# Clearing the value blocks in DRAM ahead of the key load of batch 1 instead of inside the loop: a graph-attention kernel on one Trainium2 core

## The chip, the core and the metric

The kernel runs on one core of one Trainium2 chip. The metric is the device time in microseconds (us) of one execution, as the median of three runs. Beside the runs there is one profiled execution, from which all rows and durations come. In its rows PE is TensorE (PEld its weight loads), DVE is VectorE, ACT is ScalarE, POOL is GpSimd and SP is SyncE, which here only issues DMAs.

## The reference

Sixteen batches (B = 16) of N = 512 nodes with F = 512 features go through a graph attention in two directions (`adj` as it is and transposed), with H = 16 heads of 32 features. Only the first 20 nodes (`NONGT`) serve as keys and values. All is float32.

```python
q_exp = where(row_zero, 0, q)                       # row_zero: x.sum(-1) == 0
self_feat = concat([x, q_exp]) @ W_self.T + b_self
out = self_feat
for d in range(2):
    A = adj (d == 0) or its transpose, [:, :, :20, :]       # 11 labels
    cond, vb = A.sum(-1), A @ w_bias + b_bias
    kv = self_feat[:, :20]
    aff = (self_feat @ Wq.T + bq) . (kv @ Wk.T + bk) / sqrt(32)   # per head
    w = softmax(where(cond > 0, aff, -9e15) + vb)
    out = out + (w @ kv) @ Wout[head].T + bout
return x + relu(out)
```

## The kernel before

**Set-up.** The first 92 us load all weights and compute, for all 16 batches at once, what hangs only on the 320 key nodes: `keys` (L551) makes from keys and query weights one matrix per batch, 512 x 640 (16 heads x 40 columns: 20 nodes in 2 directions), and writes it to DRAM: `g1_d` for batch 1 (L585), `g_d` for batches 2 to 15 (L586); that of batch 0 stays in SBUF (`g0`). `values` (L525) makes the values times the output weights and writes them to `vw_d`.

**Value blocks.** The attention weights of a node tile are turned with 32x32 transposes, so a head's 40 columns do not lie on the borders of the blocks of 32. `bd_d` in DRAM holds, for each batch, the values laid out to fit: 32 rows, 4 heads of a group, 2 blocks each, 128 numbers. The rows that hold no value of the head must be zero. `clear_blocks` (L121) writes those zeros for all batches, in six DMAs (L129) of 128 to 384 pieces of 512 bytes, 768 KB in all. `blocks` (L134) copies the values from `vw_d` into the other rows, in twelve DMAs (L145) of the same pieces. The two write different rows. `load_values` (L113) reads the blocks of one batch into SBUF in four DMAs (L117).

**The loop.** It runs over the batches b, and in each over four tiles of 128 nodes, nt = 0 to 3. All engines follow the order in which the program was written (`manual_schedule`); nothing is sorted by a planner. For a tile:

- PE: `self_feat` (L189) parts of this batch or the next, 16 matmuls each, into a bank of the pool `ps_acc`, which has four banks; then `scores` (L254), 32 matmuls with the keys of the batch (`load_keys`, L111); in nt = 2 of every batch b > 0 also `attend` (L321) for batch b - 1, 128 small matmuls with `vd`, which need all four banks of `ps_acc`.
- DVE: `self_copy` (L202) empties a `self_feat` bank into SBUF, `weigh` (L265, L267, L269) adds masks and subtracts the maximum, `normal` (L301, L302) sums, `turn` (L310) transposes. For the masks, `mask_count` (L216, L217) counts labels and `mask_add` (L223, L225) adds the bias.
- ACT: exponentials (L274), `mask_mul` (L210) turns the integer masks into floats, copies (L230).
- POOL: multiplies masks by the label weights (L211), adds masks and key bias (`full_add`, L239), scales the exponentials (L303).

The masks of a batch come in two halves, `adj(b,0)` and `adj(b,1)` (L96); the bias of keys is `cq(b)` (L103, two DMAs). In b = 1 the first work on `adj(1,1)` is in nt = 0.

**The DMA queue of SP.** Nearly all transfers are issued by SP, in program order. Around the change the order is: the last writes of `g1_d` and `g_d`; then, at the head of the loop, the keys of batch 1; in b = 0, nt = 1 `adj(1,0)`, `cq(1)`, the six clears, the twelve blocks; in nt = 2 the values of batch 0, `x(2)` (L88), `adj(1,1)`, two halves of `xn(2)` (L92), then `adj(2,0)` and `cq(2)`. The lines of the program:

```python
if nt == 1:
    if b + 1 < B:
        load_adj(b + 1, 0)
        load_cq(b + 1)
    if b == 0:
        clear_blocks(zero)
        blocks()
if nt == 2:
    load_values(b)
```

Each DMA signals its end on one of eight semaphores, taken in turn.

Of the kernel before, what the change touches and what calls it, by code (L numbers as in the profile page):

```python
# [18 lines left out]
def gat_kernel(  # L19
# [53 lines left out]
    zero = const.tile([32, P], F32, name="zero")  # L73
# [20 lines left out]
    def load_adj(b, h):  # L94
        t = adjs[b, h] = load.tile([P, 2, S * L], I32, tag="adj", name=f"adj{b}_{h}", bufs=3)
        nc.sync.dma_start(  # L96
            t, adj[b, h * 2 * P : (h + 1) * 2 * P].rearrange("(t p) d m l -> p t (d m l)", p=P)
        )

    def load_cq(b):  # L100
        cqs[b] = load.tile([P, H // 2, S], F32, tag="cq", name=f"cq{b}")
        for a in range(2):
            nc.sync.dma_start(  # L103
                cqs[b][bass.ts(a, R)].rearrange("p h m -> p (h m)"),
                cq_d[b : b + 1, bass.ts(a, H // 2)].rearrange("b h d m -> b (h d m)").partition_broadcast(R),
            )

    def load_keys(b):
        gs[b] = gp.tile([P, C, W], F32, tag="g", name=f"g{b}")
        src = g1_d if b == 1 else g_d[:, :, b - 2]  # L110
        nc.sync.dma_start(gs[b].rearrange("p c (a w) -> p (c a) w", a=C), src.rearrange("x p w -> p x w"))  # L111
# [9 lines left out]
    def clear_blocks(zero):  # L121

        for e in range(HL):
            for i in range(2):
                j = (e * S) // 32 + i
                lo, hi = max(e * S, 32 * j) - 32 * j, min(e * S + S, 32 * j + 32) - 32 * j
                for a, z in ((0, lo), (hi, 32)):
                    if a < z:
                        nc.sync.dma_start(  # L129
                            bb[:, a:z, e, i].rearrange("b r w -> r b w"),  # L130
                            zero[: z - a].unsqueeze(1).to_broadcast([z - a, B, P]),
                        )

    def blocks():  # L134

        vv = vw_d.rearrange("d (b m) (e w) -> d b m e w", m=NG, e=HL)
        for e in range(HL):
            for i in range(2):
                j = (e * S) // 32 + i
                for d in range(2):  # L140
                    lo = max(e * S + d * NG, 32 * j)
                    hi = min(e * S + (d + 1) * NG, 32 * j + 32)
                    if lo < hi:
                        m, r = lo - e * S - d * NG, lo - 32 * j
                        nc.sync.dma_start(bb[:, r : r + hi - lo, e, i], vv[d, :, m : m + hi - lo, e])  # L145
# [506 lines left out]

    gs[0] = g0
    with tc.manual_schedule():
        load_keys(1)

        def side(t, lo, hi, q):
# [16 lines left out]
        for b in range(B):  # L674
# [13 lines left out]
            for nt in range(NT):  # L688
                store()
                if nt == 1:  # L690
                    if b + 1 < B:
                        load_adj(b + 1, 0)
                        load_cq(b + 1)
                    if b == 0:
                        clear_blocks(zero)
                        blocks()
                if nt == 2:
                    load_values(b)
# [182 lines left out]
```

## Time and profile before

| | |
|---|---|
| runs | 630.17, 630.88, 630.75 us: median 630.75 |
| profiled execution | 630.1 us, its span (first to last instruction) 627.1 us |
| granted TensorE clock | 1.00 |
| PE busy | 619.6 us (99%) |
| DVE busy | 506.2 us (81%) |
| POOL busy | 342.1 us (55%) |
| ACT busy | 217.9 us (35%) |
| chain that ended last | PE 97%, DMA 1% |
| SP's DMA queue | 128.61 MB, 61.8% of what 16 DMA engines can do in the span |

A row of the timeline has the start and the duration in us (of all instructions that it merges), engine, line, operation, output<-inputs, shapes, the number of instructions, and in brackets the idle time of the engine before it with what ended it. SP's rows are the time that it takes to issue a DMA; the transfer goes on behind it, and the time from issue to landing is given apart.

### The profile page before, as it was taken

To read this page: it belongs to the slowest core of one execution; us is meant where nothing else is said; L and a number is where in the kernel's file an instruction comes from. 1 tells how busy PE (TensorE), PEld (TensorE's weight loads), DVE (VectorE), ACT (ScalarE), POOL (GpSimd) and SP (SyncE) were. 2 spreads that over 40 slices of the span, in tenths; PEclk is the share of its full clock that TensorE was granted. 3 is DMA by queue.
4 is the path that set the end of the run, shared out by engine and by line. 5 is a ranking of instruction groups with operands and counts; after the bars stand their busy time and mean duration, and the time that the engine had idled before them with its cause. 6 is when DMAs were issued, how large, how long until landed. Compare 5 with 4: busy or idle time off the path is not lost.

```text
span 627.1 us, 16412 instructions
## 1 busy us (share of the span) xinstructions
PE 619.6 (99%) x6830; PEld 380.3 (61%) x6830; DVE 506.2 (81%) x809; ACT 217.9 (35%) x480; POOL 342.1 (55%) x268
## 2 busy tenths in 40 slices
PE   8999999999999999999999999999999999999997
PEld 6654558866565656565565656565656565655654
DVE  1377657789888888888888979798888888888896
ACT  1445422133242424241524334332424242415341
POOL 2406332537556474738292847465564747382974
PEclk9999999999999999999999999999999999999999
DMA  8999998629284655738391919393757657492513
GB/s 303 399 393 320 360 389 247 219 76 304 102 251 154 188 219 120 286 97 310 56 350 33 334 45 290 112 289 116 232 174 186 220 135 271 87 320 49 184 36 135
DMA packets 88976, 131.53 MB, mean 210 GB/s; under 512 B 8808, under 2 KB 59016, under 8 KB 86856
## 3 DMA queue, kind: packets, MB, share of 16 engines
q1 hardware_dynamic: 87656, 128.61, 61.8%
q0 software_dynamic: 672, 1.36, 0.9%
q8 instruction: 53, 0.87, 0.6%
q10 hardware_dynamic: 576, 0.53, 0.3%
q14 instruction: 19, 0.16, 0.1%
HBM read 90.89 MB, written 39.92 MB: 209 GB/s over the span
## 4 chain that ended last, share of the span: by engine, by line
PE 97%; DMA 1%; issue 0%; SPq 0%; DVE 0%; ACT 0%; DVEq 0%
PE ps_s L254 44%; PE ps_sf L189 34%; PE ps_o L321 7%; PE ps_v L533 3%; PE ps_k L480 3%; DMA ws_q<-in_wsT 1%; PE ps_kv L431 1%; PE ps_o L667 1%; PE ps_nz L172 0%; PE ps_c L511 0%; PE ps_g(0, 3, 0, 0, 2)0_367 L560 0%; PE ps_q L441 0%; PE ps_g(1, 3, 1, 0, 2)0_530 L560 0%; PE ps_g(1, 1, 0, 1, 2)0_436 L560 0%; PE ps_g(3, 3, 0, 0, 2)0_799 L560 0%
## 5 line engine op out<-in xcount | busy, mean ns | idle before, releaser
L254 PE MATMUL ps_s<-g,sf 128*64 128x320 f32 x2048 | 287.5, 433 | 0.5 <-ACT st L575 0.5
L254 PEld LDWEIGHTS ps_s<-g,sf 128*64 128x64 f32 x2048 | 152.0, 137 | 119.9 <-issue 6.6
L189 PE MATMUL ps_sf<-x,ws_v 128*64 128x256 f32 (+1 forms) x2048 | 222.1, 371 | 0.0
L189 PEld LDWEIGHTS ps_sf<-x,ws_v 128*64 128x64 f32 x2048 | 151.5, 137 | 67.5 <-issue 2.6
L303 POOL TENSOR_TENSOR s<-s,sm 128x640 f32<-128x640 f32 x63 | 80.1, 1272 | 138.4 <-DVE sm L302 138.4
L274 ACT ACTIVATE s<-s 128x640 f32<-128x640 f32 x63 | 46.5, 738 | 214.4 <-DVE s L269 214.4
L239 POOL TENSOR_TENSOR full<-cq,both 128x640 f32<-128x640 f32 x64 | 99.0, 1547 | 25.2 <-ACT both L230 23.5
L211 POOL TENSOR_TENSOR prod<-prod,wb_sb 128x880 f32<-128x880 f32 x32 | 61.3, 1916 | 55.2 <-ACT prod L210 55.2
L265 DVE TENSOR_TENSOR ps_s<-ps_s,full 128x640 f32<-128x640 f32 x63 | 52.3, 830 | 38.6 <-PE ps_s L254 37.1
L343 POOL TENSOR_TENSOR o<-o,x 128x512 f32<-128x512 f32 x60 | 75.6, 1279 | 1.1 <-ACT o L340 1.1
L230 ACT COPY both<-add 64x80 f32<-64x80 f32 x128 | 32.8, 256 | 77.4 <-DVE add L225 76.3
L340 ACT ACTIVATE o<-o,bo 128x512 f32<-128x512 f32 x60 | 40.0, 714 | 44.3 <-DVE o L334 44.3
L301 DVE TENSOR_REDUCE sm<-s 128x32 f32<-128x640 f32 x63 | 51.6, 819 | 4.5 <-ACT s L274 0.9
L267 DVE TENSOR_REDUCE mx<-ps_s 128x32 f32<-128x640 f32 x63 | 52.0, 825 | 2.2
L269 DVE TENSOR_TENSOR s<-ps_s,mx 128x640 f32<-128x640 f32 x63 | 51.9, 824 | 2.2
L202 DVE SCALAR_TENSOR_TENSOR sf<-nz,qw,ps_sf 128x236 f32<-128x236 f32 (+1 forms) x128 | 52.6, 459 | 1.1 <-PE ps_sf L189 1.0
L310 DVE STREAM_TRANSPOSE wt<-s 128x640 f32<-128x640 f32 x63 | 52.6, 834 | 0.2 <-POOL s L303 0.2
L321 PE MATMUL ps_o<-wt,vd 32*32 32x256 f32 (+2 forms) x2176 | 45.8, 372 | 1.1 <-issue 1.1
L321 PEld LDWEIGHTS ps_o<-wt,vd 32*32 32x32 f32 x2176 | 30.2, 103 | 16.9 <-issue 8.5
L334 DVE TENSOR_TENSOR o<-ps_o,sf 128x512 f32<-128x512 f32 x60 | 36.3, 668 | 0.0
L152 ACT ACTIVATE xn<-xn 128x512 f32<-128x512 f32 x56 | 34.3, 613 | 0.0
L216 DVE TENSOR_REDUCE cond<-adj 128x80 f32<-128x880 int32 x32 | 33.2, 1037 | 1.2 <-DMA adj<-in_adj 1.2
(213 smaller groups left out, 423.1 us busy)
## 6 DMA issues: line engine op xcount, KB each, us to landing
g<-g_d SPq DMA_DIRECT2D x15, 1280.0 KB, 9.1
g_d<-st SPq DMA_DIRECT2D x16, 1120.0 KB, 6.4
x<-in_xT SPq DMA_DIRECT2D x16, 1024.0 KB, 11.0
out_T<-o SPq DMA_DIRECT2D x60, 256.0 KB, 4.3
xn<-in_xn SPq DMA_DIRECT2D x28, 512.0 KB, 8.5
adj<-in_adj SPq DMA_DIRECT2D x32, 440.0 KB, 7.2
vd<-bd_d SPq DMA_DIRECT2D x64, 128.0 KB, 4.0
nz<-nz_d SPq DMA_DIRECT2D x14, 256.0 KB, 4.9
```

The source lines that it names most:

```text
L189: nc.tensor.matmul(held[0][bass.ts(a, R), i * N // 2 : i * N // 2 + hi - lo], ws_v[:, k, bass.ds((2 * f + i) * P + a * R, R)], xs[b][:, k, ...
L202: nc.vector.scalar_tensor_tensor(sfs[b][:, 2 * f + i, lo:hi], nzs[b][:, lo:hi], qw[:, 2 * f + i, b : b + 1], ps[:, i * N // 2 : i * N // 2 ...
L211: nc.gpsimd.tensor_mul(p, p, wb_sb.unsqueeze(1).to_broadcast([P, 2 * S, L]))
L239: nc.gpsimd.tensor_add(f, cqs[b].unsqueeze(1).to_broadcast(shape), adds[b, nt // 2][:, nt % 2].unsqueeze(2).to_broadcast(shape),)
L254: nc.tensor.matmul(bank[bass.ts(a, R), : W // 2], sfs[b][:, k, bass.ds(nt * P + g * R, R)], keys[:, k, a], start=start and k == 0, stop=(k ...
L265: nc.vector.tensor_add(pw, pw, fulls.pop((b, nt)).rearrange("p g h m -> p g (h m)"))
L267: nc.vector.tensor_reduce(mx, p4, AX.X, ALU.max)
L269: nc.vector.tensor_sub(s, p4, mx.unsqueeze(3).to_broadcast(full))
L303: nc.gpsimd.tensor_mul(s, s, sm.unsqueeze(3).to_broadcast(full))
L310: nc.vector.transpose(wts[b][:, nt], s.rearrange("p a h m -> p (a h m)"))
L321: nc.tensor.matmul(banks[q][bass.ts(e, DH)].rearrange("p (t n) -> p t n", n=32), vds[b][r, e, i, q // 2 * 2 + n], wt[r, :, bass.ts(j, 32)] ...
L343: nc.gpsimd.tensor_add(o[:, c], o[:, c], xs[b][:, c])
```

## The change

`clear_blocks(zero)` is called at the head of the loop's section, before the keys of batch 1 are loaded, and no longer in b = 0, nt = 1. `blocks()` stays where it is. The six clears are the same; on SP they now stand ahead of the keys of batch 1, `adj(1,0)` and the two DMAs of `cq(1)`.

```diff
     gs[0] = g0
     with tc.manual_schedule():
+        clear_blocks(zero)
         load_keys(1)
 
         def side(t, lo, hi, q):
...
                         load_adj(b + 1, 0)
                         load_cq(b + 1)
                     if b == 0:
-                        clear_blocks(zero)
                         blocks()
                 if nt == 2:
                     load_values(b)
```

## The prediction

> **What bounds the kernel now.** First the page:
>
> ```profile
> span 627.1 us, 16412 instructions
> PE 619.6 (99%) x6830; PEld 380.3 (61%) x6830; DVE 506.2 (81%) x809; ACT 217.9 (35%) x480; POOL 342.1 (55%) x268
> ```
>
> TensorE (PE) is busy for 619.6 of 627.1 us at a granted clock of 1.00, and the chain that ended last is 97% PE. A moved DMA can therefore change the time only where PE itself stands still. From the point of the edit (92 us) on, PE's rows show one such place inside the loop, and one only (the other, 0.48 us, is in the tail): the first `attend`, of batch 0, in b = 1, nt = 2. Below it stands the same step one batch later (start us, duration us, group, idle before):
>
> ```profile
> 134.44 0.63 PE L321 MATMUL ps_o<-wt,vd 32*32 32x256 f32 x6
> 135.66 2.70 PE L321 MATMUL ps_o<-wt,vd 32*32 32x256 f32 x122 [0.58 <-issue]
> ...
> 168.94 2.75 PE L321 MATMUL ps_o<-wt,vd 32*32 32x256 f32 x128
> ```
>
> From the first `attend` matmul to the scores after it (138.28) batch 0 takes 3.84 us; one batch later it is 168.94 to 171.62, 2.68 us. The stall costs **1.16 us**. The fourth accumulator bank is what is missing: PE's sequencer waits 3.33 us in one place of L321, up to 135.60, when VectorE (DVE) has emptied that bank with the last L202. So DVE's rows come next:
>
> ```profile
> 123.37 0.35 DVE L302 RECIPROCAL sm<-sm 128x32 f32<-128x32 f32 x1
> 124.97 1.07 DVE L216 TENSOR_REDUCE cond<-adj 128x80 f32<-128x880 int32 x1 [1.25 <-DMA adj<-in_adj]
> 126.08 1.93 DVE L217 TENSOR_SCALAR cond<-cond 128x80 f32<-128x80 f32 x1
> 127.93 0.86 DVE L202 SCALAR_TENSOR_TENSOR sf<-nz,qw,ps_sf 128x256 f32<-128x256 f32 x2
> 128.71 0.82 DVE L265 TENSOR_TENSOR ps_s<-ps_s,full 128x640 f32<-128x640 f32 x1
> ...
> 134.69 0.86 DVE L202 SCALAR_TENSOR_TENSOR sf<-nz,qw,ps_sf 128x256 f32<-128x256 f32 x2
> ```
>
> From 124.97 to 135.55 DVE has no idle time. It entered this stretch late, because L216 waited 1.25 us for the masks `adj(1,1)`. And L217 took 1.93 us where the other batches show 0.51: it ended just after GpSimd's (POOL's) L211 (126.03 to 127.95), which it met only because it was late. Last the SP queue, which issues those masks:
>
> ```profile
> 92.03 0.32 SPq L586 DMA_DIRECT2D g_d<-st  x1
> 94.48 0.37 SPq L111 DMA_DIRECT2D g<-g_d  x1
> 94.91 2.27 SPq L96 DMA_DIRECT2D adj<-in_adj  x1
> 97.22 1.18 SPq L103 DMA_DIRECT2D cq<-cq_d  x2
> 98.44 6.12 SPq L129 DMA_DIRECT2D bd_d<-zero  x6
> 104.67 8.87 SPq L145 DMA_DIRECT2D bd_d<-vw_d  x12
> 116.60 1.72 SPq L117 DMA_DIRECT2D vd<-bd_d  x4
> 118.36 0.43 SPq L88 DMA_DIRECT2D x<-in_xT  x1
> 118.84 0.50 SPq L96 DMA_DIRECT2D adj<-in_adj  x1
> ```
>
> SP goes through this without a pause but two: 92.35 to 94.48, where the key load L111 waits for the last write of `g1_d`, and 113.54 to 116.60, where L117 waits for the blocks. The last row is `adj(1,1)`: issued at 118.84, landed 6.1 us later, at 124.95.
>
> **The change, part by part.** No instruction is added or removed; six DMAs (`clear_blocks`, L129) pass three loads (keys of batch 1, `adj(1,0)`, `cq(1)`: four DMAs) on SP. From the first block (L145) on the order of all queues is as before.
>
> *Clears earlier.* They need only `zero`, set at 0.7 us. They start at 92.40, in the 2.1 us in which SP waited. The program also makes each SP DMA wait for the landing of the one eight places before it; for the sixth clear that is a `g_d` write landed at 94.12, for the others it has landed by 91.5. Their SP time lies between 6 x 0.31 = 1.9 us (the shortest of the six) and the 6.12 us of before: they end between about 94.4 and 98.5.
>
> *Keys, `adj(1,0)`, `cq(1)` later.* Counted on SP, the keys are issued at 98.5 at the latest instead of 94.48: 4.0 us later. Counted on the DMA engines, which are full at that time (share 1.04 in 96 to 100, 320 GB/s), the 768 KB (786 kB) of clears go ahead: at 257 GB/s (the window 102 to 103, in which they ran before) 3.1 us, at 320 GB/s 2.5 us. I take 3.2 us, bounds 2.5 and 4.0. The keys landed before `cq(1)`, which landed at 103.3 at the latest; shifted, they come by 107, and PE first reads them at 122.21: 15 us of cover, cost nothing. `cq(1)` is read at 117.41 by POOL: nothing. `adj(1,0)`, in by 103.3 before, comes at 106.5 (105.8 to 107.3). ScalarE reads it at 107.34, DVE at 108.59; a delay there would first use up DVE's idle time of 1.48 us at 117.62. Cost nothing.
>
> [...]
>
> *Blocks earlier, with new neighbours.* Through the same rule of eight, block 5 now waits for the keys and block 6 for `adj(1,0)`, where both waited for older transfers. So SP, free for the blocks at about 101 to 102, does the first four and stops at block 5 and 6: block 6 starts with the landing of `adj(1,0)`, at 106.5. Before, the trace has it at 109.05. The blocks 6 to 12 follow at 0.60 to 0.64 us each as before, so that everything behind is **2.5 us earlier** (1.8 to 3.2): values L117, `x(2)`, and `adj(1,1)`, which lands at 122.4 (121.7 to 123.2).
>
> *What that is worth.* L216 needs its masks when the reciprocal of 123.37 is through, at 123.64. With 122.4 the 1.25 us of idle time are gone. L217 then starts at 124.7 and waits for POOL's L303 alone (to 125.14), as in later batches, not for L211; it ends at 125.2, and L202 at 126.0. L265 no longer waits for DVE but for PE's scores, which end at 126.75: it starts at 126.85 in place of 128.71, 1.86 us earlier. The rest of the stretch keeps its length (128.71 to 135.55, 6.84 us) and ends at 133.7, ahead of PE's need at 134.44. If L217 met L211 all the same (125.14 to 127.06 then), L265 would start at 127.8, 0.9 us earlier, and 0.25 us of the stall would stay. I take the first, since four later batches that I looked at have L217 at 0.51.
>
> So the stall of 1.16 us goes, and no more can be had: PE is then without a pause up to the tail. Behind it PE's chain moves as a whole, since from b = 2 on no `attend` has such a pause. SP itself next waits at 122.6 to 140.3 for the row flags of DVE, so the 2.5 us of SP end there.
>
> **Sum.** Profiled execution of before: 630.1 us, span 627.1. Minus 1.16: span 625.9, execution 628.9. The median of the three runs, 630.75, lies 0.65 above the profiled execution: 630.75 - 1.16 = **629.6 us**.
>
> **Rivals.**
>
> *A: nothing is gained.* If `adj(1,0)` lands at 109.05, block 6 and all behind stand where they stood, and the time is 630.75. Against it: that takes 5.7 us of delay, where SP's own count gives at most 4.0. For it: the four DMA issues behind the clears may be held up as L96 was (2.27 us) by 1536 packets more in the queue, and the blocks may be slower than 0.6 us while the keys still run.
>
> *B: slower, through block 6.* The mechanism is the new wait of block 6 for `adj(1,0)`: from a landing at 109.05 on, each us of delay is a us for `adj(1,1)`, for L216 and for the bank that PE waits for. It happens if the clears get through the queue at less than 786 kB / 5.7 us = 137 GB/s. In 104 to 108, when half of them ran before, the core's DMA engines moved 114 GB/s: 6.9 us, landing at 110.2, the stall 1.2 us longer, 631.9 us. At the slowest us (104 to 105, 72 GB/s) 10.9 us, landing at 114.2, 5.2 us longer, 635.9 us. Against it: in those windows the DMA share was 0.52 and 0.36, the queue waited for SP, while at 92 it is full and SP is ahead of it.
>
> That the change does not do what it says is no case: the order of SP is fixed by hand.
>
> **Numbers.** A measurement of this kernel can tell about 0.2% from no change, 1.26 us. The gain of 1.16 us stands 0.1 us short of that line, and the three runs of before spread over 0.71 us, so the main case falls on both sides almost evenly. Main case 0.75: 0.36 faster, 0.39 same. A 0.12: 0.11 same, 0.01 slower. B 0.10: 0.09 slower, 0.01 same. Left over 0.03: 0.01 faster, 0.02 slower. That makes faster 0.37, same 0.51, slower 0.12. The range starts at the main case less 0.6 for the spread, 629.0, takes in the gain of 0.9 and rival A with half the spread, 631.1, and leaves B out.
>
> **What would show it.** In the profile after: L129 from 92.4, L111 between 95 and 98.5; L145 from about 101, with a pause before its fifth or sixth DMA; L117 at about 114 in place of 116.60; no "DMA adj" in front of the L216 that follows, L217 there at 0.5 us; the first L321 in one piece of 2.7 us; a span near 625.9. Wrong it is if L117 is not at least 1.3 us earlier, if L217 still takes 1.9 us, or if PE waits at L321 though DVE is early.

## The result: 0.3% slower

The changed kernel takes 632.44 us, the kernel before 630.31 us (medians of 21 executions each). The ratio is **1.0032**, with a 95% interval of 1.0021 to 1.0043: 1.3 to 2.7 us lost, where 1.16 us of gain was forecast. The profiled execution took 632.8 us:

```profile
span 630.2 us, 16411 instructions
PE 620.2 (98%) x6830; PEld 380.8 (60%) x6830; DVE 507.8 (81%) x809; ACT 218.5 (35%) x480; POOL 342.4 (54%) x268
```

PE's busy time has grown by 0.6 us only; the span by 3.1. The rows of PE at the first `attend` show nearly all of it (start, duration, group, idle before):

```profile
134.70 0.63 PE L321 MATMUL ps_o<-wt,vd 32*32 32x256 f32 x6
137.45 4.03 PE L321 MATMUL ps_o<-wt,vd 32*32 32x256 f32 x122 [2.13 <-issue]
```

The stall has not gone but grown, from 0.58 to 2.13 us of idle time. And the 122 matmuls behind it take 4.03 us in place of 2.70. The table by stage tells why (us, then busy time and instructions of PE, PEld, DVE, ACT and POOL, then the granted clock of PE, the DMA share and GB/s):

```profile
136.00:138.00 2.00, 0.55 (x32) 0.35 (x33) 1.98 (x4) 1.02 (x4) 0.68 (x2) 0.94 0.00 0
138.00:141.00 3.00, 3.00 (x107) 2.26 (x89) 2.50 (x4) 1.09 (x2) 1.33 (x1) 0.50 0.03 5
...
141.00:142.00 1.00, 1.00 (x26) 0.34 (x6) 0.10 (x2) 0.87 (x4) 0.00 (x0) 0.92 0.00 0
```

Behind the longer stall the granted clock is 0.50 for some 3.4 us. So the 3.1 us are: 1.55 of stall, 1.33 of half clock, and 0.26 that this execution was late already at the end of set-up (its first `scores` begin at 91.90, those of before at 91.65). The half clock does not come in every execution. A mean clock of 0.997 or less, as in the profiled one, is found in 9 of the 21; their median is 633.43 us, that of the other twelve 631.39. So about 1.1 us of the loss is there without it.

VectorE is late twice, and each time L217 meets POOL's L211 and takes 1.92 us. In batch 0, where the kernel before has neither a wait nor a long L217, L216 now waits too. First the kernel before, in batch 0:

```profile
108.59 1.01 DVE L216 TENSOR_REDUCE cond<-adj 128x80 f32<-128x880 int32 x1
109.64 0.51 DVE L217 TENSOR_SCALAR cond<-cond 128x80 f32<-128x80 f32 x1
```

Then the changed one, DVE in both batches and POOL's two L211:

```profile
110.93 1.07 DVE L216 TENSOR_REDUCE cond<-adj 128x80 f32<-128x880 int32 x1 [2.00 <-DMA adj<-in_adj]
112.03 1.92 DVE L217 TENSOR_SCALAR cond<-cond 128x80 f32<-128x80 f32 x1
...
126.78 1.07 DVE L216 TENSOR_REDUCE cond<-adj 128x80 f32<-128x880 int32 x1 [0.82 <-DMA adj<-in_adj]
127.88 1.92 DVE L217 TENSOR_SCALAR cond<-cond 128x80 f32<-128x80 f32 x1
...
136.49 0.86 DVE L202 SCALAR_TENSOR_TENSOR sf<-nz,qw,ps_sf 128x256 f32<-128x256 f32 x2
```
```profile
111.99 1.91 POOL L211 TENSOR_TENSOR prod<-prod,wb_sb 128x880 f32<-128x880 f32 x1 [1.64 <-ACT prod L210]
...
127.84 1.91 POOL L211 TENSOR_TENSOR prod<-prod,wb_sb 128x880 f32<-128x880 f32 x1 [0.45 <-ACT prod L210]
```

And SP, where it begins:

```profile
92.65 8.54 SPq L129 DMA_DIRECT2D bd_d<-zero  x6
101.29 0.94 SPq L111 DMA_DIRECT2D g<-g_d  x1
102.27 2.83 SPq L96 DMA_DIRECT2D adj<-in_adj  x1
105.14 1.48 SPq L103 DMA_DIRECT2D cq<-cq_d  x2
106.73 9.46 SPq L145 DMA_DIRECT2D bd_d<-vw_d  x12
118.35 1.73 SPq L117 DMA_DIRECT2D vd<-bd_d  x4
```

The clears hold SP for 8.54 us, against 6.12 in their old place; each of the six takes 0.99 to 1.88 us. The keys go out at 101.3, 6.8 us later than before. `adj(1,0)` is issued 7.4 us later (102.27 for 94.91) and lands at 110.9. The blocks start 2.1 us later than before instead of some 3 us earlier, and L117 is 1.75 us later.

What the DMA engines did meanwhile is in two rows, of the kernel before and of the changed one:

```profile
96.00:104.00 8.00, 8.00 (x68) 7.00 (x66) 5.91 (x9) 1.76 (x5) 1.53 (x2) 1.00 0.99 303
```
```profile
96.00:104.00 8.00, 8.00 (x68) 6.99 (x66) 5.91 (x9) 1.76 (x5) 1.27 (x2) 1.00 0.61 143
```

Before, the 2048 pieces of the keys, with `adj(1,0)` and `cq(1)` behind them, kept the engines full (0.99, 303 GB/s) while SP was issuing the small clears. With the clears in front, the same eight microseconds move less than half (0.61, 143 GB/s), and the keys' transfer comes after them.

### The profile page after: what moved, and what is told of

Read it like the earlier page. It is cut to its first block, busy times and chain, and to the rows that moved or that the text cites. A ratio compares the mean times of both kernels' runs of the same rounds, so it can differ in the third digit from the quotient of the medians.

```text
span 630.2 us, 16411 instructions
## 1 busy us (share of the span) xinstructions
PE 620.2 (98%) x6830; PEld 380.8 (60%) x6830; DVE 507.8 (81%) x809; ACT 218.5 (35%) x480; POOL 342.4 (54%) x268
## 4 chain that ended last, share of the span: by engine, by line
PE 97%; DMA 1%; issue 0%; SPq 0%; DVE 0%; ACT 0%; DVEq 0%
PE ps_s L254 44%; PE ps_sf L189 34%; PE ps_o L321 7%; PE ps_v L533 3%; PE ps_k L480 3%; DMA ws_q<-in_wsT 1%; PE ps_kv L431 1%; PE ps_o L668 1%; PE ps_nz L172 0%; PE ps_c L511 0%; PE ps_g(0, 3, 0, 0, 2)0_367 L560 0%; PE ps_q L441 0%; PE ps_g(1, 0, 1, 0, 2)0_415 L560 0%; PE ps_g(3, 2, 0, 1, 2)0_773 L560 0%; PE ps_g(3, 0, 1, 1, 2)0_718 L560 0%
## 5 line engine op out<-in xcount | busy, mean ns | idle before, releaser
L211 POOL TENSOR_TENSOR prod<-prod,wb_sb 128x880 f32<-128x880 f32 x32 | 61.3, 1916 | 56.5 <-ACT prod L210 56.4
L343 POOL TENSOR_TENSOR o<-o,x 128x512 f32<-128x512 f32 x60 | 75.6, 1280 | 1.1 <-ACT o L340 1.1
L321 PE MATMUL ps_o<-wt,vd 32*32 32x256 f32 (+2 forms) x2176 | 47.1, 384 | 2.4 <-issue 2.4
L216 DVE TENSOR_REDUCE cond<-adj 128x80 f32<-128x880 int32 x32 | 33.3, 1040 | 2.8 <-DMA adj<-in_adj 2.8
```

Of the source, the lines that this page charges most:

```text
L211: nc.gpsimd.tensor_mul(p, p, wb_sb.unsqueeze(1).to_broadcast([P, 2 * S, L]))
L321: nc.tensor.matmul(banks[q][bass.ts(e, DH)].rearrange("p (t n) -> p t n", n=32), vds[b][r, e, i, q // 2 * 2 + n], wt[r, :, bass.ts(j, 32)] ...
L343: nc.gpsimd.tensor_add(o[:, c], o[:, c], xs[b][:, c])
```

## The experiments

Two theories at first. *Theory 1 (late masks):* all of it goes through SP: the clears make SP and `adj(1,0)` late, with them the blocks, the values and `adj(1,1)`, and so the bank that PE waits for. *Theory 2 (late DVE):* `adj(1,0)` alone makes DVE late in batch 0, and that stays. In the edits below, "before" and "changed" name the kernel that was edited. The first four ran on one chip beside 35 executions of the kernel before (630.93 us), the next four beside 35 others (630.90), the last beside 11 (630.71).

**c_early_masks**: changed, `adj(1,1)` ahead of the blocks.

```diff
                     if b == 0:
+                        load_adj(1, 1)
                         blocks()
...
-                    if b + 1 < B:
+                    if 0 < b < B - 1:
                         load_adj(b + 1, 1)
```

> The changed kernel with adj(1,1) issued right behind cq(1), ahead of the blocks. Theory 1 (late masks): the clears at the head delay adj(1,0), block 6 waits for its landing (110.9 us), all behind is 1.8 us late, adj(1,1) lands at 126.8, DVE empties the fourth bank late and PE stands still at the first attend. With adj(1,1) early the stall is gone, and with it the half clock behind it: about 629.2, 1.2 below the kernel before, 3.2 below the changed one. Theory 2 (late DVE): DVE is late already in batch 0, since L216 waits 2.0 us for adj(1,0) and L217 then meets L211; adj(1,1) only hides that. Then DVE starts L216 of batch 1 at 125.9, ends the last L202 at about 135.0, and PE still stands 0.3 to 1.0 us: 629.5 to 630.3.

Measured: 629.75 us, ratio 0.9986 (0.9972 to 1.0000). The clears still hold SP for 7.47 us, and L216 of batch 0 still waits 2.18 us, but L216 of batch 1 no longer waits, L217 takes 0.51, and the first `attend` is one piece of 3.26 us:

```profile
111.81 1.07 DVE L216 TENSOR_REDUCE cond<-adj 128x80 f32<-128x880 int32 x1 [2.18 <-DMA adj<-in_adj]
...
126.75 1.01 DVE L216 TENSOR_REDUCE cond<-adj 128x80 f32<-128x880 int32 x1
127.80 0.51 DVE L217 TENSOR_SCALAR cond<-cond 128x80 f32<-128x80 f32 x1
```

So most of the loss goes with `adj(1,1)`, as theory 1 has it. But DVE's rows are those of theory 2: L216 of batch 1 starts at 126.75, where theory 2 had 125.9 (0.7 us between them because set-up ended later here). The time doesn't tell them apart: 629.75 lies in theory 2's range, and it is 1.2 us below the kernel before beside it, as theory 1 has it. Theory 2's part is what is left, some 0.5 us of that piece against 2.75 in other batches.

**b_early_masks**: before, with `adj(1,1)` issued at the same place, here ahead of the clears too. It prices the stall alone.

> The kernel before with adj(1,1) issued right behind cq(1), ahead of the clears and blocks. This prices the stall by itself: L216 of batch 1 without a wait, L217 at 0.5 us, the first attend in one piece of 2.7 us. Theory 1: 1.16 us less than before, 629.15. If PE waits there for something else (the values, POOL), 630.3.

Measured: 629.41 us, ratio **0.9974** (0.9964 to 0.9984), the first version that is clearly faster than both kernels:

```profile
123.84 1.01 DVE L216 TENSOR_REDUCE cond<-adj 128x80 f32<-128x880 int32 x1
124.89 0.52 DVE L217 TENSOR_SCALAR cond<-cond 128x80 f32<-128x80 f32 x1
```
```profile
134.65 2.76 PE L321 MATMUL ps_o<-wt,vd 32*32 32x256 f32 x128
```

This is to the row what the prediction described for the changed kernel: no wait, no meeting with L211, no stall. The valuation of the stall held; its 1.16 us are 0.18%, at the low end of the interval of 0.16 to 0.36%.

**b_late_masks**: before, `adj(1,1)` behind one half of `xn(2)`, and the clears untouched.

```diff
-                    if b + 1 < B:
+                    if 0 < b < B - 1:
                         load_adj(b + 1, 1)
                     if b + 2 < B:
                         load_xn(b + 2, 0)
+                        if b == 0:
+                            load_adj(1, 1)
                         load_xn(b + 2, 1)
```

> The kernel before with adj(1,1) issued behind the first half of xn(2): 512 KB more ahead of it, 1.3 us, and 0.5 us of issue, so that it lands about 1.8 us later, as in the changed kernel; adj(1,0), the clears and the blocks are untouched. Theory 1: the stall at the first attend grows from 1.2 to about 3 us, with a half clock behind it in part of the executions (up to 1.35 us): 632.0 to 633.4. Theory 2: adj(1,0) is on time, so most of the loss stays away: 630.3 to 631.0.

Measured: 632.80 us, ratio 1.0032 (1.0018 to 1.0047), the loss of the changed kernel without any of its edit. L216 waits 2.26 us, PE 1.59:

```profile
127.04 1.07 DVE L216 TENSOR_REDUCE cond<-adj 128x80 f32<-128x880 int32 x1 [2.26 <-DMA adj<-in_adj]
```
```profile
137.72 2.69 PE L321 MATMUL ps_o<-wt,vd 32*32 32x256 f32 x122 [1.59 <-issue]
```

Theory 1 has its price: a late `adj(1,1)` is enough for a loss of this size, with the clears in their old place.

**c_masks10_first**: changed, `adj(1,0)` ahead of the clears.

```diff
+        load_adj(1, 0)
         clear_blocks(zero)
         load_keys(1)
...
                     if b + 1 < B:
-                        load_adj(b + 1, 0)
+                        if b > 0:
+                            load_adj(b + 1, 0)
                         load_cq(b + 1)
```

> The changed kernel with adj(1,0) ahead of the clears. Both theories: L216 of batch 0 finds its masks, and DVE is on time there. Theory 1: block 6 now waits for the keys, which land at about 108.5 instead of 110.9 for adj(1,0); the blocks are then 0.5 to 1 us ahead of the kernel before, adj(1,1) lands about 124.3, and the stall is 0.3 to 1.2 us long: 629.4 to 630.3. Theory 2: the delay came from adj(1,0) alone, so the time is that of the kernel before or 0.3 less, 630.0 to 630.3. Were the clears slow for everything behind them whatever the order, it would stay at 632.

Measured: 631.45 us, ratio 1.0021 (1.0003 to 1.0038). A miss for both theories as I had put them. DVE was on time in batch 0 (no wait at L216), which speaks against theory 2; but the loss stayed, though no block waited for a transfer any more. SP was simply late: clears 8.00 us, keys at 100.87, `cq(1)` held for 5.08 us behind them, blocks from 107.28:

```profile
92.77 8.00 SPq L129 DMA_DIRECT2D bd_d<-zero  x6
100.87 1.18 SPq L111 DMA_DIRECT2D g<-g_d  x1
102.09 5.08 SPq L103 DMA_DIRECT2D cq<-cq_d  x2
107.28 8.17 SPq L145 DMA_DIRECT2D bd_d<-vw_d  x12
117.65 1.72 SPq L117 DMA_DIRECT2D vd<-bd_d  x4
```

Counted from the first `scores` (91.55 here, 91.65 before, 91.90 changed), L117 comes 1.15 us later than in the kernel before, where the changed kernel has 1.50. So the waits of blocks 5 and 6 are only a part of what costs. In the changed kernel SP's waits say the same:

```profile
SPq L145 <- DMA adj<-in_adj: 0.5, 1, 0.5
SPq L145 <- DMA g<-g_d: 0.5, 1, 0.5
```

1.0 us together, part of which only takes the place of waits at L117 (2.8 us before, 1.9 now). Open was then why the clears take longer at the head, and why that reaches the blocks. Two answers were tried (they are not the prediction's rivals A and B): *theory A*, some DMA engines carry too many of the pieces and hold SP back; *theory B*, each issue has a price of its own.

**c_even_clears** and **b_even_clears**: the same bytes, with the batches as the outer dimension, in the changed kernel and in the one before.

```diff
-                            bb[:, a:z, e, i].rearrange("b r w -> r b w"),
-                            zero[: z - a].unsqueeze(1).to_broadcast([z - a, B, P]),
+                            bb[:, a:z, e, i],
+                            zero[:B].unsqueeze(1).to_broadcast([B, z - a, P]),
```

> The changed kernel with the same bytes cleared in an order with the 16 batches outermost, so that each clear is spread over all 16 DMA engines. Before, the trace counts 8, 12 or 16 engines that signal the end of a clear, by its rows; the busiest engines carry 128 of the 1536 pieces, spread evenly they would carry 96. Theory A (the engines hold the issue back): SP's time for the six clears falls from 8.5 to about 6.4 us, adj(1,0) lands 2 us earlier, at about 109, and the time is that of the kernel before within 0.4: 630.5 to 631.3, where the kernel before has 630.9. Theory B (each issue has a fixed price of some 1.4 us): 8.5 us stay, and the loss of 0.2 to 0.4% stays: 632.2 to 633.0.

> The kernel before with the clears spread over 16 engines in the same way, in their old place. Theory A: SP's stretch from the clears to the blocks gets about 1.5 us shorter, adj(1,1) lands by 123.6, the stall at the first attend goes: about 1.2 us less than before, 629.5 to 629.9. Theory B: no change, 630.9.

Measured: 632.33 us, ratio 1.0021 (1.0001 to 1.0041), and 630.46 us, ratio 0.9984 (0.9965 to 1.0003). The pieces now lie as those of the blocks do, each of which ends with 16 signals in the trace of the kernel before, where its clears end with 8, 12 or 16. Yet SP needs 7.34 us at the head, little less than in c_early_masks with the old order (7.47); in the old place it is 5.57 against 6.12. So the order of the pieces does not explain the 8.54 us, and theory A is not borne out. The second ratio can't be told from 1.

**c_half_clears**: changed, half the batches at the head, the others in b = 1.

```diff
-    def clear_blocks(zero):
+    def clear_blocks(zero, lo_b, hi_b):
...
-                            bb[:, a:z, e, i].rearrange("b r w -> r b w"),
-                            zero[: z - a].unsqueeze(1).to_broadcast([z - a, B, P]),
+                            bb[lo_b:hi_b, a:z, e, i].rearrange("b r w -> r b w"),
+                            zero[: z - a].unsqueeze(1).to_broadcast([z - a, hi_b - lo_b, P]),
...
-        clear_blocks(zero)
+        clear_blocks(zero, 0, B // 2)
         load_keys(1)
...
                     if b == 0:
                         blocks()
+                    if b == 1:
+                        clear_blocks(zero, B // 2, B)
```

> The changed kernel with the clears of batches 0 to 7 alone at the head (384 KB), and those of batches 8 to 15 behind cq(2) in b = 1, nt = 1, where SP waits anyway. Theory A: half the pieces, 4 to 5 us of SP at the head, adj(1,0) lands at about 107, the blocks start 1.5 to 2 us earlier than in the kernel before, the stall goes: 629.4 to 629.8. Theory B: still six issues, 8.5 us, 632.2 to 633.0.

Measured: 629.68 us, ratio **0.9968** (0.9950 to 0.9986).

```profile
93.33 5.38 SPq L129 DMA_DIRECT2D bd_d<-zero  x6
98.80 0.39 SPq L111 DMA_DIRECT2D g<-g_d  x1
...
103.24 8.64 SPq L145 DMA_DIRECT2D bd_d<-vw_d  x12
```

Six issues with half the pieces take 5.4 us, not 8.5: theory B is out as a fixed price. The blocks start 10.0 us after the last issue of set-up has ended (93.27 here), where the kernel before needs 12.3 (92.35 to 104.67) and the changed one 14.1 (92.60 to 106.73). PE has no stall. So the clears at the head cost nothing in this run, at 5.38 us. Whether the head is what gains is not shown: the other half now stands behind the blocks, and half the clears in the old place was not run. In time this can't be told from b_early_masks; in both the one stall is gone, and the first `attend` is one piece of 2.76 us.

**c_keys_first**: changed, with the keys ahead of the clears again.

```diff
-        clear_blocks(zero)
         load_keys(1)
+        clear_blocks(zero)
```

> The changed kernel with the keys of batch 1 ahead of the clears: the clears pass adj(1,0) and cq(1) alone, and SP waits again for g1_d ahead of the keys. If the filled wait of 2.1 us is all that the move has on its good side, this is slower than the changed kernel by up to 2 us: adj(1,0) at 110 to 113, stall of 2 to 4 us, 632 to 635. If the clears are slow because they stand directly behind the g_d writes, they take some 6 us here as in the kernel before, blocks start at about 105, and the time is 630.9 to 631.8.

Measured: 631.37 us, ratio 0.9994 (0.9977 to 1.0011): level with the kernel before. One place in the queue, and the loss of 0.3% is not seen any more, although the clears still pass `adj(1,0)` and `cq(1)` and SP again waits ahead of the keys, here 1.0 us.

```profile
93.80 0.37 SPq L111 DMA_DIRECT2D g<-g_d  x1
94.22 7.92 SPq L129 DMA_DIRECT2D bd_d<-zero  x6
102.18 1.43 SPq L96 DMA_DIRECT2D adj<-in_adj  x1
...
105.73 7.79 SPq L145 DMA_DIRECT2D bd_d<-vw_d  x12
```
```profile
96.00:104.00 8.00, 8.00 (x69) 7.04 (x66) 5.91 (x9) 1.76 (x5) 1.27 (x1) 1.00 0.90 253
```

The clears take about as long on SP (7.92 us), but now the keys' transfer runs beneath them: the share in 96 to 104 is back at 0.90, 253 GB/s. The blocks start 1.0 us earlier than in the changed kernel and, without the waits of blocks 5 and 6, take SP 7.79 us in place of 9.46. So the order of keys and clears is the cause of the loss. The keys cost SP 0.37 us and the engines some four (an estimate: 1280 KB at 303 GB/s, as in 96 to 104 of the kernel before, to 338, as in 104 to 108 of the changed one); the clears cost SP 6 to 8.5 us and leave the engines partly idle (a share of 0.70 in 96 to 98 and 0.41 in 100 to 102 of the changed kernel). In the old order one hides the other, in the new one they add up. The time fits the second case of the expectation, but its reason failed: the clears did not get shorter. What sets the 1 to 1.9 us of one clear's issue is not settled: neither the order of the pieces, nor a fixed price, nor the place directly behind the `g_d` writes.

**b_later_masks**: before, `adj(1,1)` behind both halves of `xn(2)`, for the clock.

```diff
-                    if b + 1 < B:
+                    if 0 < b < B - 1:
                         load_adj(b + 1, 1)
                     if b + 2 < B:
                         load_xn(b + 2, 0)
                         load_xn(b + 2, 1)
+                    if b == 0:
+                        load_adj(1, 1)
```

> The kernel before with adj(1,1) issued behind both halves of xn(2): 1 MB more ahead of it, 2.6 us, and some 1.2 us of issue. In the profiled executions so far the stall of PE at the first attend was 2.2 us long at most without a loss of clock (c_masks10_first, b_late_masks) and had a half clock of 3.4 us behind it once, at 2.7 us (the changed kernel). Theory C (a long stall of PE brings the half clock): the stall is 4 to 5 us here, the half clock comes in nearly all executions, mean clock 0.994 to 0.998, and the time is 3 to 3.6 us of stall plus 1 to 2 us of clock above the kernel before: 635 to 637. Without C: 634 to 634.6, clock as in the kernel before.

Measured: 635.47 us, ratio 1.0069 (1.0048 to 1.0090). PE stands still for 2.90 us, less than expected, and the 122 matmuls behind take 4.46 us:

```profile
136.00:140.00 4.00, 0.85 (x22) 0.40 (x38) 3.88 (x8) 2.35 (x9) 1.27 (x1) 0.80 0.00 0
140.00:144.00 4.00, 4.00 (x122) 2.51 (x116) 2.89 (x4) 1.81 (x5) 1.54 (x1) 0.50 0.02 4
144.00:148.00 4.00, 4.00 (x34) 1.93 (x26) 3.67 (x8) 1.04 (x4) 1.27 (x1) 0.84 0.19 17
```

The mean clock is 0.994 to 0.997 in all six executions. Theory C holds for this stall.

All profiled executions but one together, counted from the first `scores` of the loop so that the set-up drops out:

| kernel | L216 of b = 1 starts after | idle of PE at the first `attend` | ratio |
|---|---|---|---|
| b_early_masks | 31.99 us | none | 0.9974 |
| c_half_clears | 31.99 us | none | 0.9968 |
| c_keys_first | 32.92 us | 0.18 us | 0.9994 |
| before | 33.32 us | 0.58 us | 1 |
| b_even_clears | 33.48 us | 0.73 us | 0.9984 |
| b_late_masks | 34.34 us | 1.59 us | 1.0032 |
| c_even_clears | 34.35 us | 1.61 us | 1.0021 |
| c_masks10_first | 34.56 us | 1.80 us | 1.0021 |
| changed | 34.88 us | 2.13 us | 1.0032 |
| b_later_masks | 36.05 us | 2.90 us | 1.0069 |

(c_early_masks stands apart: its L216 starts after 34.15 us with the masks there, and then saves L217's 1.4 us.) Whatever is done to the queue, PE's idle time follows the moment at which the first work on `adj(1,1)` begins, and so does the time, within its intervals.

## Why the prediction was wrong

- *What bounds the kernel, and what the stall is worth*: right. PE's stall at the first `attend`, from `adj(1,1)` over L216 and L217 to the fourth bank; b_early_masks removed it as described.
- *Clears earlier*: this term was mis-sized. Its bounds, 1.9 us and the 6.12 us of before, did not hold: it measured 8.54 us, 7.3 to 8.5 in the four kernels with all clears at the head of the loop ahead of the keys. I took the old place's issue time as the worst case. Why it is longer at the head stays open: in c_keys_first the keys stand ahead of the clears again, and they still take 7.92.
- *Keys, `adj(1,0)`, `cq(1)` later*: the step that failed, by the same error. I took 3.2 us, at most 4.0. It rested on 786 kB at 257 GB/s, a rate read from one microsecond in which other transfers ran too. `adj(1,0)` came at 110.9, 7.8 us after the 103.1 of before (by its semaphore's record in the trace), and 7.4 of the 7.8 are its later issue: from issue to landing it took 8.6 us, 8.2 before. The engines were not full meanwhile (143 GB/s at a share of 0.61 with all that ran). So the delay arose in SP's issue of the clears, not in the data rate that I counted with. (`cq(1)`, read as landed by 103.3, landed at 103.6; nothing hangs on it.) That `adj(1,0)`'s delay would cost nothing was wrong as well: DVE lost 2.00 us there and 1.4 more at L217; c_early_masks puts its own share at some 0.5 us.
- *Blocks earlier*: followed from it, with the wrong sign: the blocks start 2.1 us later, and L117 behind them 1.75. The waits of blocks 5 and 6 did appear, 0.5 us each.
- *Rival B* is nearest to what happened: it had the landing at 110.2 (measured 110.9) and the time 1.2 us longer (measured 2.1, of which about 1.1 without the half clock). That is luck in part. Its mechanism did act: block 6 started with the landing of `adj(1,0)`, 1.9 us later than before. But its delay came from a data rate, and c_masks10_first lost without that wait, since SP itself was late. Against it I had held that "at 92 it is full and SP is ahead of it". In the changed kernel the DMA share is 1.01 in 92 to 96, 0.70 in 96 to 98 and 0.41 in 100 to 102: from 96 on SP is behind.
- The half clock, 1.33 us in the profiled execution, stood in no case.

## What to carry to other kernels

On one queue, put the transfer that is long for the DMA engines and short for the issuer ahead of the ones that are short for the engines and long for the issuer: the issue of the second kind then runs beneath the first, as in c_keys_first (a share of 0.90 in 96 to 104, where the changed kernel has 0.61). Here that order alone undid the loss (ratio 0.9994 with the keys first, 1.0032 with the clears first). The wait of 2.1 us on this queue could hide 2.1 us of what was put into it, and not 8.54. And the issue time read at one place of the queue was no bound for another: the six clears took SP 5.5 to 6.1 us at their old place and 7.3 to 8.5 at the head.

## What the runs showed of the hardware

A pause of TensorE cost more than its length here. Behind 2.13 us of idle (the changed kernel) the granted clock went to 0.50 for 3.4 us, and the 122 matmuls took 4.03 us in place of 2.70; behind 2.90 us (b_later_masks) it went to 0.50 for about 6.8 us. Behind 1.59 to 1.80 us the profiled executions show none: the 122 matmuls took 2.69 to 2.70 us. By the mean clocks it comes in part of the executions. 3.4 us at 0.50 take 0.003 off the mean clock of an execution, so a mean of 0.997 or less is counted as a sign of it:

| kernel | idle of PE at the first `attend` (profiled) | mean clock of 0.997 or less |
|---|---|---|
| b_later_masks | 2.90 us | 6 of 6 |
| changed | 2.13 us | 9 of 21 |
| c_masks10_first | 1.80 us | 2 of 12 |
| c_even_clears | 1.61 us | 6 of 12 |
| b_late_masks | 1.59 us | 6 of 12 |
| b_even_clears | 0.73 us | 2 of 11 |
| before | 0.58 us | 8 of 81 (2 of 35, 5 of 35, 1 of 11) |
| c_keys_first | 0.18 us | 0 of 11 |
| c_early_masks | none | 1 of 12 |
| b_early_masks, c_half_clears | none | 0 of 23 |

So kernels with idle times of about 1.6 us show this sign too, in half of their executions (6 of 12, twice). That fits the spread of the changed kernel, 628.85 to 635.12 us, beside 627.99 to 631.53 for the 21 of the kernel before; another 35 of that kernel, five of them with such a clock, spread from 629.38 to 635.35.

Not expected either: a DVE instruction on 80 numbers in each of 128 partitions (L217) took 0.20 to 0.52 us or 1.92 to 1.93 us in the loop of the two kernels' profiles. Each of the three long ones began 0.04 to 0.05 us behind an L211 of POOL (1.91 to 1.92 us) and ended some 0.05 us behind its end; no short one began while an L211 ran. In the other nine profiles the L217 of batch 1 took 1.92 to 1.93 us where L216 had waited for its masks (0.84 to 3.98 us), and 0.51 to 0.52 us where it had not. In the changed kernel a DMA that landed 0.82 us late so cost VectorE 1.41 us more.
